# One-row projections of a non-local block as column tiles, with batch statistics from one row per image

## The chip, the cores and the metric

The kernel runs on one NeuronCore of a Trainium2 chip. The metric is device time in microseconds (us) for one execution, the median of several runs. The core has a matrix engine (TensorE, PE), two engines for elementwise work (VectorE, DVE; ScalarE, ACT), GpSimd (POOL) and DMA queues. Tensors in the on-chip memory have 128 partitions; a matmul writes to a separate memory, PSUM[...].

## The reference

The whole kernel is four layers on x of shape (4, 256, 32, 32) in float32: a state-space block, the block treated here, attention with a mixture of experts, and attention with a recurrence of 1024 steps. The change is in layer 1 alone. With N = H*W = 1024 pixels and C = 256 channels it computes

```
g_x     = conv1x1(x, g_w, g_b)          # one output channel: (B, N, 1)
theta_x = conv1x1(x, theta_w, theta_b)  # (B, N, 1)
phi_x   = conv1x1(x, phi_w, phi_b)      # (B, 1, N)
f = matmul(theta_x, phi_x) / N
y = matmul(f, g_x)                      # = theta * (sum over n of phi*g) / N
w_y = conv1x1(y, w_w, w_b)              # C channels: w_w[c]*y + w_b[c]
mean, var = over batch and pixels, per channel
w_y = (w_y - mean) * rsqrt(var + EPS) * bn_gamma + bn_beta
return w_y + x
```

theta, phi and g have one channel each, so y of an image is its theta times one number d, the dot product of phi and g over N. w_y of channel c is then a multiple of that row plus a constant.

## The kernel before, in words

x lies in memory as [128, C=2, B=4, L=1024]: channel c*128+p of image b on partition p. `PHASES` (L1612) calls `_setup`, `_layer0`, `_layer1`, `_layer2`, `_layer3`. A tile framework schedules the instructions of each engine by their dependencies and inserts the semaphores; an engine runs its own list strictly in order. Only the recurrence of layer 3 has an order written out by hand (`_in_order`). Pools of tiles are stacked, so a pool opened by a later phase can lie on memory that an earlier phase has given back; its first writer then waits for the last user.

Layer 0 ends in `_out_and_se` (L439): the pooled mean (L478, L481), two small matmuls (L484, L489), a sigmoid (L491), and L493, eight VectorE instructions of 1024 columns, channel half by channel half and image by image, that add the result to x. ScalarE then issues the load of layer 2's weights, w_l (`_weights`, L178).

`_layer1` (L499) has three steps.

- Projections. L510 spreads each of the six weight columns over 128 columns, so that the matmul (L521) puts the single output channel on all 128 partitions. Eight blocks of W=512 columns, three names and two halves of the contraction make 48 matmuls of 512 columns. ScalarE adds the biases to theta (L525, into y) and phi (L529), and VectorE multiplies g + g_b by phi with an accumulator for the dot product (L530).
- Scaling. The dot products of the two blocks of an image are added (L534, L535) and y of each image is multiplied by its number (L537).
- Batch norm and residual, for each channel half: ScalarE makes w_y over all 4096 columns (L543); `_batchnorm` (L555) takes bn_stats of the eight blocks (L561), aggregates them (L563), and forms scale (L565 to L567); VectorE normalises w_y (L548) and adds it with bn_beta to x (L549).

`_layer2_attention` (L652) follows. `_layernorm` (L184) forms the mean over channels by a matmul with a constant matrix (L196), subtracts it (L197), squares (L199), sums the squares by a matmul (L201), takes a root (L209) and a reciprocal (L211), spreads it by a matmul (L215) and multiplies (L216). `_layer2_weights` (L571) multiplies attention weights into each other (L596, L600, L602) and copies the results (L583 and L603 to L610): these need no x, and the scheduler places them where their inputs allow. `_layer2` prepares constants by small VectorE and POOL instructions (L634 to L644). `_rsqrt` (L911) is a chain of small VectorE instructions, a first guess and four Newton rounds (L930, L932, L934); layers 0 and 2 call it before the change.

A column tile is a matmul with 32 output rows at `tile_position=(0, 32*i)`; it uses 32 of the array's 128 columns and writes PSUM partitions 32*i to 32*i+31. The router in `_head` (L787) and the input gates of layer 3 (L1500) are written in that way already.

Of the kernel before, what the change touches and what calls it, by code (L numbers as in the profile page):

```python
# [10 lines left out]
F32 = mybir.dt.float32  # L11
U32 = mybir.dt.uint32
I32 = mybir.dt.int32
AF = mybir.ActivationFunctionType
ALU = mybir.AluOpType
AX = mybir.AxisListType
PSUM = bass.MemoryType.PSUM

P = 128
B = 4  # L20
L = 1024
T = B * L
D = 256
C = D // P
W = 512
NBLK = T // W
BPI = L // W
# [43 lines left out]
def _bc(ap, axis, n):  # L71

    a = ap.unsqueeze(axis)
    shape = list(a.shape)
    shape[axis] = n
    return a.to_broadcast(shape)
# [421 lines left out]

def _layer1(s):  # L499

    nc, tc = s.nc, s.tc
    with ExitStack() as ctx:
        keep = ctx.enter_context(tc.tile_pool(name="l1_keep", bufs=1))
        pool = ctx.enter_context(tc.tile_pool(name="l1", bufs=2))
        ps = ctx.enter_context(tc.tile_pool(name="l1_ps", bufs=2, space=PSUM))
        wide = {}
        for name in ("theta", "phi", "g"):
            wide[name] = keep.tile([P, C, P], F32, name=f"{name}_wide")
            for k in range(C):
                nc.vector.tensor_scalar_mul(  # L510
                    wide[name][:, k, :], s.ones, s.col[f"{name}_w"][:, k : k + 1]
                )
        y = keep.tile([P, B, L], F32, name="y")
        dot = keep.tile([P, NBLK], F32, name="dot")
        for i in range(NBLK):
            b, t0 = divmod(i * W, L)
            p = {}
            for name in ("theta", "phi", "g"):
                p[name] = ps.tile([P, W], F32, name=f"p_{name}")
                for k in range(C):  # L520
                    nc.tensor.matmul(  # L521
                        p[name], wide[name][:, k, :], s.xt[:, k, bass.ts(i, W)],
                        start=k == 0, stop=k == C - 1,
                    )
            nc.scalar.activation(  # L525
                y[:, b, t0 : t0 + W], p["theta"], AF.Identity, bias=s.row["theta_b"]
            )
            phi = pool.tile([P, W], F32, name="phi")
            nc.scalar.activation(phi, p["phi"], AF.Identity, bias=s.row["phi_b"])  # L529
            nc.vector.scalar_tensor_tensor(  # L530
                phi, p["g"], s.row["g_b"], phi, ALU.add, ALU.mult, accum_out=dot[:, i : i + 1]
            )
        dots = keep.tile([P, B], F32, name="dots")
        nc.vector.tensor_reduce(dots, dot.rearrange("p (b i) -> p b i", i=BPI), AX.X, ALU.add)  # L534
        nc.vector.tensor_scalar_mul(dots, dots, 1.0 / L)  # L535
        for b in range(B):
            nc.vector.tensor_scalar_mul(y[:, b, :], y[:, b, :], dots[:, b : b + 1])  # L537

        yt = y.rearrange("p b l -> p (b l)")
        for c in range(C):  # L540
            wy = pool.tile([P, NBLK, W], F32, name="wy")
            wyt = wy.rearrange("p i w -> p (i w)")
            nc.scalar.activation(  # L543
                wyt, yt, AF.Identity,
                bias=s.col["w_b"][:, c : c + 1], scale=s.col["w_w"][:, c : c + 1],
            )
            mean, scale = _batchnorm(s, pool, wy, s.col["bn_gamma"][:, c : c + 1])
            nc.vector.tensor_scalar(wyt, wyt, mean, scale, ALU.subtract, ALU.mult)  # L548
            nc.vector.scalar_tensor_tensor(  # L549
                s.xt[:, c, :], wyt, s.col["bn_beta"][:, c : c + 1], s.xt[:, c, :],  # L550
                ALU.add, ALU.add,
            )


def _batchnorm(s, pool, v, gamma):  # L555

    nc = s.nc
    n = v.shape[1]
    stats = pool.tile([P, n, nc.vector.BN_STATS_DIM], F32, name=f"bn_stats{n}")
    for i in range(n):  # L560
        nc.vector.bn_stats(stats[:, i, :], v[:, i, :])  # L561
    mv = pool.tile([P, 2], F32, name=f"bn_mv{n}")
    nc.vector.bn_aggr(mv, stats.rearrange("p n d -> p (n d)"))  # L563
    scale = pool.tile([P, 1], F32, name=f"bn_scale{n}")
    nc.scalar.activation(scale, mv[:, 1:2], AF.Sqrt, bias=s.eps)  # L565
    nc.vector.reciprocal(scale, scale)
    nc.vector.tensor_mul(scale, scale, gamma)  # L567
    return mv[:, 0:1], scale
# [772 lines left out]
def _layer3_lstm(s, x, u_l3, lam, add_col):  # L1341
# [269 lines left out]

PHASES = [  # L1612
    _setup, _layer0, _layer1, _layer2, _layer3,
]

# [88 lines left out]
```

## Time and profile before

| | |
|---|---|
| median of three runs | 3567.6 us (3564.02 to 3568.08) |
| the profiled execution | 3564.65 us |
| its span | 3562.9 us |
| busy share of the span | PE 91%, PE weight load 72%, DVE 57%, ACT 35%, POOL 12% |
| mean granted TensorE clock | 0.965 |
| layer 0's last addition to x (L493) | 357.28 to 366.94 us |
| projections of layer 1 (L521) | from 367.28 us |
| y scaled (L537), w_y (L543) | from 411.98 us, from 414.81 us |
| last residual of layer 1 (L549) | from 438.95 us, 4.48 long |
| layer 2's layernorm, first subtraction (L197) | 445.60 us |

A row of the timeline gives the start, the time that the instructions took, engine, line, operation, output and input tiles, and in brackets how long the engine had idled and what released it. A float32 matmul of 512 columns appears as two records. In windows, the numbers are busy time and instructions of PE, PE weight load, DVE, ACT and POOL, then the granted clock, the DMA share and GB/s.

### The profile page before, as it was taken

The numbers are of one execution on the slowest core, as the hardware profiler recorded it, in microseconds if no ns is written. First come the engines' busy times: TensorE is split into PE (matmuls) and PEld (weight loads), VectorE is DVE, ScalarE is ACT, GpSimd is POOL, SyncE is SP. The second block draws the span as 40 slices with busy tenths as digits, with TensorE's granted clock in tenths as the row PEclk, the third lists the DMA queues.
The fourth block names the chain that finished last, engine by engine and source line by source line (L and its number), as shares of the span: only waits on it lengthen the run. The fifth ranks groups of instructions, "written<-read, shape, count | busy, mean of one in ns | idle before, by whom it ended". The sixth has DMA issues, their size and how long they took to land.

```text
span 3562.9 us, 146932 instructions
## 1 busy us (share of the span) xinstructions
PE 3253.3 (91%) x65426; PEld 2549.0 (72%) x65426; DVE 2028.1 (57%) x8373; ACT 1249.5 (35%) x5057; POOL 416.0 (12%) x498
## 2 busy tenths in 40 slices
PE   7786599998899999589999999999999999999888
PEld 4464234445788888357888888888888888888776
DVE  5795544443211111536677777776777777777666
ACT  4623222222222222233334334343343343343333
POOL 0181000113433333200000000000000000000000
PEclk9898789999999999799999999999999999999999
DMA  1390000114455654300000000000000000000000
GB/s 66 88 293 1 9 0 12 36 36 157 175 193 212 223 194 160 125 1 4 5 5 10 4 10 4 5 10 4 4 10 4 10 4 4 10 4 5 10 4 10
DMA packets 79356, 189.32 MB, mean 53 GB/s; under 512 B 6592, under 2 KB 64256, under 8 KB 73728
## 3 DMA queue, kind: packets, MB, share of 16 engines
q0 software_dynamic: 16176, 116.06, 8.9%
q1 hardware_dynamic: 60624, 59.12, 5.6%
q8 instruction: 512, 8.39, 1.0%
q10 hardware_dynamic: 1920, 4.74, 0.4%
q14 instruction: 124, 1.02, 0.1%
HBM read 118.88 MB, written 61.02 MB: 50 GB/s over the span
## 4 chain that ended last, share of the span: by engine, by line
PE 41%; DVE 9%; ACT 4%; issue 2%; ACTq 0%; DVEq 0%
PE p_c L1556 10%; DVE turned L1585 7%; PE p_c L1547 7%; PE p_i L1547 4%; PE p_o L1547 4%; PE p_o L1556 4%; PE p_i L1556 4%; PE beside L1500 4%; ACT a_o L1586 2%; DVE x L1601 2%; ACT th L1599 2%; PE beside L1404 1%; PE beside L1441 0%; PE var L1451 0%; PE p_q L1324 0%
## 5 line engine op out<-in xcount | busy, mean ns | idle before, releaser
L1586 ACT ACTIVATE add<-turned 128x8 f32<-128x8 f32 x1024 | 214.4, 209 | 1027.3 <-DVE turned L1585 1027.3
L1556 PE MATMUL p_c<-w_v,x 128*4 128x64 f32 x16368 | 416.1, 219 | 71.0 <-DVE x L1601 69.0
L1547 PE MATMUL p_c<-xg,shift 128*128 128x64 f32 x2048 | 445.7, 299 | 0.0
L1556 PE MATMUL p_o<-w_v,x 128*4 128x64 f32 x16368 | 416.3, 219 | 0.0
L1556 PE MATMUL p_i<-w_v,x 128*4 128x64 f32 x16368 | 416.1, 219 | 0.0
L1547 PE MATMUL p_i<-xg,shift 128*128 128x64 f32 x2048 | 407.3, 281 | 0.0
L1585 DVE STREAM_TRANSPOSE turned<-p_c 128x64 f32<-128x64 f32 x1024 | 255.7, 250 | 259.0 <-PE p_c L1556 228.0
L1547 PE MATMUL p_o<-xg,shift 128*128 128x64 f32 x2048 | 396.1, 275 | 0.0
L1547 PEld LDWEIGHTS p_c<-xg,shift 128*128 128x128 f32 x2048 | 304.7, 188 | 117.6 <-issue 0.3
L1556 PEld LDWEIGHTS p_c<-w_v,x 128*4 128x4 f32 x16368 | 227.2, 85 | 192.3 <-DVE x L1601 119.1
L1547 PEld LDWEIGHTS p_o<-xg,shift 128*128 128x128 f32 x2048 | 310.9, 192 | 0.3
L1601 DVE TENSOR_TENSOR x<-a_o,th 128x8 f32<-128x8 f32 x1024 | 170.8, 167 | 244.2 <-ACT th L1599 244.2
L1547 PEld LDWEIGHTS p_i<-xg,shift 128*128 128x128 f32 x2048 | 304.7, 188 | 0.4 <-issue 0.3
L1127 PE MATMUL ph<-uT,w 128*128 128x256 f32 x1248 | 282.7, 384 | 16.8 <-DVE uT L1112 12.5
L1141 PE MATMUL po<-w,hT 128*128 128x256 f32 x1248 | 285.5, 382 | 5.6 <-issue 5.0
L1131 ACT ACTIVATE hT<-ph,w 128x256 f32<-128x256 f32 x312 | 147.6, 473 | 398.5 <-PE ph L1127 369.4
L1556 PEld LDWEIGHTS p_o<-w_v,x 128*4 128x4 f32 x16368 | 281.1, 87 | 0.1
L1556 PEld LDWEIGHTS p_i<-w_v,x 128*4 128x4 f32 x16368 | 280.9, 87 | 0.0
L1127 PEld LDWEIGHTS ph<-uT,w 128*128 128x128 f32 x1248 | 238.4, 192 | 54.3 <-DVE uT L1112 16.3
L1585 DVE STREAM_TRANSPOSE turned<-p_i 128x64 f32<-128x64 f32 x1024 | 271.7, 265 | 0.3 <-PE p_i L1547 0.3
L1141 PEld LDWEIGHTS po<-w,hT 128*128 128x128 f32 x1248 | 236.0, 192 | 37.3 <-issue 5.4
L1148 DVE TENSOR_TENSOR y<-po,w 128x256 f32<-128x256 f32 x78 | 33.0, 423 | 392.9 <-PE po L1141 369.6
(409 smaller groups left out, 4678.7 us busy)
## 6 DMA issues: line engine op xcount, KB each, us to landing
sorted<-zeros SPq DMA_DIRECT2D x32, 1032.0 KB
y_in<-results SPq DMA_DIRECT2D x16, 512.0 KB
x<-in_x_dram SPq DMA_DIRECT2D x8, 512.0 KB
tokens<-rows SPq DMA_DIRECT2D x4, 1024.0 KB
x<-tokens SPq DMA_DIRECT2D x8, 512.0 KB
out_dram<-x_l SPq DMA_DIRECT2D x64, 64.0 KB
results<-y,place POOLq DMA_INDIRECT x78
w_l<-in_w_l_dram ACTq DMA_DIRECT2D x1, 1092.0 KB
```

Source lines behind the costliest of these rows:

```text
L1127: nc.tensor.matmul(ph, w1[:, k, bass.ts(n, P)], uT[:, k, :], start=k == 0, stop=k == C - 1,)
L1131: nc.scalar.activation(hT[:, n, :], ph, AF.Gelu, bias=b1[:, n : n + 1])
L1141: nc.tensor.matmul(po, hT[:, n, bass.ts(a, P)], w2[:, n, :], start=n == 0, stop=n == NHC - 1,)
L1148: nc.vector.tensor_add(y, po, b2)
L1404: nc.tensor.matmul(p, lam[:, k, b, bass.ts(m, P)], u_l3[:, k, b * L + n * SB : b * L + (n + 1) * SB], start=k == 0, stop=k == C - 1,)
L1500: nc.tensor.matmul(p[bass.ts(i, R), :], rows[:, k, bass.ts(g, R)], w_u[:, k, at : at + GQ // GC], start=k == 0, stop=k == C - 1, tile_posi ...
L1547: nc.tensor.matmul(p[:, :H], shift[:, row * B : row * B + P], xg[n][:, g, bass.ts(i, H)], start=True, stop=t == 0,)
L1556: nc.tensor.matmul(p[R * i : R * i + B, :H], hs[:, t - 1, bass.ts(k, B)], w_v[:, k, i * GQ + g * H : i * GQ + (g + 1) * H], start=False, s ...
L1585: nc.vector.transpose(zt.rearrange("p c w -> p (c w)"), pz[g][:, :H])
L1586: nc.scalar.activation(dst.rearrange("p (c b) -> p c b", c=C), zt[:, :, :B], f)
L1599: nc.scalar.activation(th, cell[:, :, 1], AF.Tanh)
L1601: nc.vector.tensor_mul(h, a_o, th)
```

## The change

`_layer1` is rewritten; `_batchnorm` stays in use in layer 3.

- theta, phi and g of an image are rows of column tiles. w holds two sets of 32 columns for each half of the contraction: theta and phi in columns 0 and 1 of the first, g in column 1 of the second. Image b goes to column tile b. For each half i of the pixels, p_0 gets theta and phi, p_1 gets g, of all four images: 2 x 2 x 2 x 4 = 32 matmuls of 512 columns. p_0 and p_1 have one PSUM buffer each.
- ScalarE adds both biases in one instruction to rows; bn_stats runs on rows, so that each image's theta row yields mean and variance; VectorE multiplies p_1 + g_b by rows with an accumulator.
- The dot product, mean and variance of each image are placed in columns of own and summed over partitions by a matmul with ones, which gives them to all partitions (every).
- From these, d, the batch mean and the variance of w_y follow by arithmetic on 4 or 2 columns; `_rsqrt` takes the root. coef and off hold each channel's factor for each image and its constant.
- For each image, a matmul with spread puts its theta row on all partitions, in PSUM; ScalarE forms w_y from it with scale and bias (two instructions of 1024 columns), and VectorE adds it to x.

The diff:

```diff
 def _layer1(s):
 
+
     nc, tc = s.nc, s.tc
+    R = P // B
     with ExitStack() as ctx:
         keep = ctx.enter_context(tc.tile_pool(name="l1_keep", bufs=1))
         pool = ctx.enter_context(tc.tile_pool(name="l1", bufs=2))
-        ps = ctx.enter_context(tc.tile_pool(name="l1_ps", bufs=2, space=PSUM))
-        wide = {}
-        for name in ("theta", "phi", "g"):
-            wide[name] = keep.tile([P, C, P], F32, name=f"{name}_wide")
-            for k in range(C):
-                nc.vector.tensor_scalar_mul(
-                    wide[name][:, k, :], s.ones, s.col[f"{name}_w"][:, k : k + 1]
+        ps = ctx.enter_context(tc.tile_pool(name="l1_ps", bufs=1, space=PSUM))
+        wide = ctx.enter_context(tc.tile_pool(name="l1_wide", bufs=2, space=PSUM))
+
+        w = keep.tile([P, 2, C, R], F32, name="w")
+        nc.vector.memset(w, 0.0)
+        for held, row, name in ((0, 0, "theta"), (0, 1, "phi"), (1, 1, "g")):
+            nc.vector.tensor_copy(w[:, held, :, row], s.col[f"{name}_w"])
+        at = s.ident.rearrange("p (b r) -> p r b", r=R)
+        bias = keep.tile([P, 1], F32, name="bias")
+        on = keep.tile([P, 2], F32, name="on")
+        nc.vector.tensor_reduce(on, at[:, :2, :], AX.X, ALU.add)
+        nc.vector.tensor_scalar_mul(bias, on[:, :1], s.row["theta_b"])
+        nc.vector.scalar_tensor_tensor(
+            bias, on[:, 1:], s.row["phi_b"], bias, ALU.mult, ALU.add
+        )
+        spread = keep.tile([P, B, P], F32, name="spread")
+        nc.vector.tensor_copy(spread, _bc(at[:, 0, :], 2, P))
+        w_sq = keep.tile([P, C], F32, name="w_sq")
+        nc.vector.tensor_mul(w_sq, s.col["w_w"], s.col["w_w"])
+
+        rows = keep.tile([P, BPI, W], F32, name="rows")
+        stats = keep.tile([P, BPI, nc.vector.BN_STATS_DIM], F32, name="stats")
+        dot = keep.tile([P, BPI], F32, name="dot")
+        for i in range(BPI):
+            p = [ps.tile([P, W], F32, name=f"p_{j}") for j in range(2)]
+            for j in range(2):
+                for k in range(C):
+                    for b in range(B):
+                        nc.tensor.matmul(
+                            p[j][bass.ts(b, R), :], w[:, j, k, :], s.x[:, k, b, bass.ts(i, W)],
+                            start=k == 0, stop=k == C - 1, tile_position=(0, R * b),
+                        )
+            nc.scalar.activation(rows[:, i, :], p[0], AF.Identity, bias=bias)
+            nc.vector.bn_stats(stats[:, i, :], rows[:, i, :])
+            prod = pool.tile([P, W], F32, name="prod")
+            nc.vector.scalar_tensor_tensor(
+                prod, p[1], s.row["g_b"], rows[:, i, :], ALU.add, ALU.mult,
+                accum_out=dot[:, i : i + 1],
+            )
+        mv = keep.tile([P, 2], F32, name="mv")
+        nc.vector.bn_aggr(mv, stats.rearrange("p n d -> p (n d)"))
+
+        own = keep.tile([P, 3, B], F32, name="own")
+        nc.vector.tensor_scalar_mul(own[:, 0, :], at[:, 1, :], dot[:, :1])
+        for i in range(1, BPI):
+            nc.vector.scalar_tensor_tensor(
+                own[:, 0, :], at[:, 1, :], dot[:, i : i + 1], own[:, 0, :], ALU.mult, ALU.add
+            )
+        for i in range(2):
+            nc.vector.tensor_scalar_mul(own[:, 1 + i, :], at[:, 0, :], mv[:, i : i + 1])
+        p = ps.tile([P, 3, B], F32, name="p_own")
+        nc.tensor.matmul(
+            p.rearrange("p q b -> p (q b)"), s.ones, own.rearrange("p q b -> p (q b)"),
+            start=True, stop=True,
+        )
+        every = keep.tile([P, 3, B], F32, name="every")
+        nc.vector.tensor_copy(every, p)
+        d = keep.tile([P, B], F32, name="d")
+        nc.vector.tensor_scalar_mul(d, every[:, 0, :], 1.0 / L)
+
+        dm = keep.tile([P, B], F32, name="dm")
+        nc.vector.tensor_mul(dm, d, every[:, 1, :])
+        mean = keep.tile([P, 1], F32, name="mean")
+        nc.vector.tensor_reduce(mean, dm, AX.X, ALU.add)
+        nc.vector.tensor_scalar_mul(mean, mean, 1.0 / B)
+        nc.vector.tensor_scalar(dm, dm, mean, None, ALU.subtract)
+        nc.vector.tensor_mul(dm, dm, dm)
+        dv = keep.tile([P, B], F32, name="dv")
+        nc.vector.tensor_mul(dv, d, d)
+        nc.vector.tensor_mul(dv, dv, every[:, 2, :])
+        nc.vector.tensor_add(dv, dv, dm)
+        var = keep.tile([P, 1], F32, name="var")
+        nc.vector.tensor_reduce(var, dv, AX.X, ALU.add)
+        var_c = keep.tile([P, C], F32, name="var_c")
+        nc.vector.tensor_scalar(var_c, w_sq, var, 1.0 / B, ALU.mult, ALU.mult)
+        gain = keep.tile([P, C], F32, name="gain")
+        for _ in _rsqrt(s, pool, gain, var_c):
+            pass
+        nc.vector.tensor_mul(gain, gain, s.col["bn_gamma"])
+        scale = keep.tile([P, C], F32, name="scale")
+        nc.vector.tensor_mul(scale, gain, s.col["w_w"])
+        coef = keep.tile([P, B, C], F32, name="coef")
+        nc.vector.tensor_mul(coef, _bc(d, 2, C), _bc(scale, 1, B))
+
+        off = keep.tile([P, C], F32, name="off")
+        nc.vector.scalar_tensor_tensor(
+            off, s.col["w_w"], mean, s.col["w_b"], ALU.mult, ALU.add
+        )
+        nc.vector.tensor_sub(off, s.col["w_b"], off)
+        nc.vector.tensor_mul(off, off, gain)
+        nc.vector.tensor_add(off, off, s.col["bn_beta"])
+
+        for b in range(B):
+            theta = wide.tile([P, BPI, W], F32, name="theta")
+            for i in range(BPI):
+                nc.tensor.matmul(
+                    theta[:, i, :], spread[:, b, :], rows[:, i, :], start=True, stop=True
                 )
-        y = keep.tile([P, B, L], F32, name="y")
-        dot = keep.tile([P, NBLK], F32, name="dot")
-        for i in range(NBLK):
-            b, t0 = divmod(i * W, L)
-            p = {}
-            for name in ("theta", "phi", "g"):
-                p[name] = ps.tile([P, W], F32, name=f"p_{name}")
-                for k in range(C):
-                    nc.tensor.matmul(
-                        p[name], wide[name][:, k, :], s.xt[:, k, bass.ts(i, W)],
-                        start=k == 0, stop=k == C - 1,
-                    )
-            nc.scalar.activation(
-                y[:, b, t0 : t0 + W], p["theta"], AF.Identity, bias=s.row["theta_b"]
-            )
-            phi = pool.tile([P, W], F32, name="phi")
-            nc.scalar.activation(phi, p["phi"], AF.Identity, bias=s.row["phi_b"])
-            nc.vector.scalar_tensor_tensor(
-                phi, p["g"], s.row["g_b"], phi, ALU.add, ALU.mult, accum_out=dot[:, i : i + 1]
-            )
-        dots = keep.tile([P, B], F32, name="dots")
-        nc.vector.tensor_reduce(dots, dot.rearrange("p (b i) -> p b i", i=BPI), AX.X, ALU.add)
-        nc.vector.tensor_scalar_mul(dots, dots, 1.0 / L)
-        for b in range(B):
-            nc.vector.tensor_scalar_mul(y[:, b, :], y[:, b, :], dots[:, b : b + 1])
-
-        yt = y.rearrange("p b l -> p (b l)")
-        for c in range(C):
-            wy = pool.tile([P, NBLK, W], F32, name="wy")
-            wyt = wy.rearrange("p i w -> p (i w)")
-            nc.scalar.activation(
-                wyt, yt, AF.Identity,
-                bias=s.col["w_b"][:, c : c + 1], scale=s.col["w_w"][:, c : c + 1],
-            )
-            mean, scale = _batchnorm(s, pool, wy, s.col["bn_gamma"][:, c : c + 1])
-            nc.vector.tensor_scalar(wyt, wyt, mean, scale, ALU.subtract, ALU.mult)
-            nc.vector.scalar_tensor_tensor(
-                s.xt[:, c, :], wyt, s.col["bn_beta"][:, c : c + 1], s.xt[:, c, :],
-                ALU.add, ALU.add,
-            )
+            for c in range(C):
+                wy = pool.tile([P, L], F32, name="wy")
+                nc.scalar.activation(
+                    wy, theta.rearrange("p i w -> p (i w)"), AF.Identity,
+                    bias=off[:, c : c + 1], scale=coef[:, b, c : c + 1],
+                )
+                xs = s.x[:, c, b, :]
+                nc.vector.tensor_add(xs, xs, wy)
 
 
 def _batchnorm(s, pool, v, gamma):
```

## The prediction

> **What bounds the kernel now.** I first read the table of windows for the stretch between the end of layer 0 and layer 2's layernorm, then its timeline.[...]
>
> ```profile
> 366.90:372.00 5.10, 4.72 (x7) 2.15 (x8) 1.21 (x7) 0.69 (x1) 0.00 (x0) 0.58 0.00 0
> 372.00:411.70 39.70, 38.78 (x92) 16.90 (x90) 6.19 (x17) 10.30 (x15) 0.00 (x0) 1.00 0.00 0
> 411.70:443.50 31.80, 7.37 (x29) 4.46 (x29) 27.45 (x46) 9.36 (x5) 0.18 (x1) 0.62 0.00 0
> ...
> 447.00:473.10 26.10, 26.04 (x64) 7.53 (x64) 8.72 (x11) 8.37 (x8) 0.00 (x0) 1.00 0.00 0
> ```
>
> Layer 1 has two parts, each with one engine full: TensorE to 411.7 (43.5 of 44.8 us), then VectorE (27.5 of 31.8). The ends of the parts are in the timeline (start, us, engine, line):
>
> ```profile
> 357.28 9.66 DVE L493 SCALAR_TENSOR_TENSOR x<-o,att,x 128x1024 f32<-128x1024 f32 x8 [2.42 <-ACT att L491]
> ...
> 410.79 0.75 DVE L530 SCALAR_TENSOR_TENSOR phi<-p_g,rows,phi 128x512 f32<-128x512 f32 x1 [4.39 <-PE p_g L521]
> ...
> 414.81 7.49 ACT L543 ACTIVATE wy<-y,cols 128x4096 f32<-128x4096 f32 x2 [5.12 <-DVE y L537]
> ...
> 427.32 2.40 DVE L548 TENSOR_SCALAR wy<-wy,bn_mv,bn_scale 128x4096 f32<-128x4096 f32 x1
> ...
> 438.95 4.48 DVE L549 SCALAR_TENSOR_TENSOR x<-wy,cols,x 128x4096 f32<-128x4096 f32 x1
> ...
> 445.60 2.52 DVE L197 TENSOR_TENSOR u<-x,mean 128x1024 f32<-128x1024 f32 x2 [0.60 <-PE mean L196]
> ```
>
> From layer 0's last residual (357.28 + 9.66 = 366.94) to layernorm's first subtraction (445.60) are **78.7 us**, and nothing else runs beside them: POOL has 0.35 us of work, the DMA share is 0.00. Everything later needs x, so what this stretch loses or gains goes to the end of the span.
>
> Prices come from the answer on the tile wg (durations min/median/max, first and last start) and from the groups, with shapes kept apart (count, busy us, mean ns):
>
> ```profile
> L787 PE MATMUL p_head<-x,wg x16: 379/379/403, 889.1 to 889.8; 128*32 128x256 f32 x16
> ```
>
> ```profile
> L241 ACT ACTIVATE acc<-xbc,cols 128x1024 f32<-128x1024 f32 x16 | 19.7, 1238 | 0.3
> ```
>
> ```profile
> L197 DVE TENSOR_TENSOR u<-x,mean 128x1024 f32<-128x1024 f32 x8 | 9.8, 1221 | 15.2 <-PE mean L196 15.1
> ...
> L932 DVE TENSOR_TENSOR e<-e,rstd 128x8 f32<-128x8 f32 x32 | 5.3, 166 | 1.1
> ```
>
> The first is the router's matmul in column tiles: a source matmul is two records, so 8 matmuls of 256 columns are 16 records. Full-width records of 512 columns follow each other at 0.43 us (L521), so 256 columns cost 0.215 and 16 in a row 3.4 us; they start within 0.7 us and end after 1.07. Four column tiles do run abreast.
>
> [...] granted clock 0.51 while VectorE adds the residual (357.3 to 366.9), 1.00 from 372. [...]
>
> **The change part by part**, on the clock of the profiled run (before: 366.94 to 445.60).
>
> *Preparation.* Eight small VectorE instructions (w, on, spread, bias, w_sq) stand in the built order between pooled and the first L493. VectorE idled 2.42 us there. One 128x512 copy (0.42 at L605), two of about 0.17 and five of 0.15 to 0.2 make 1.8, and the memset of w waits some 0.5 us for TensorE to let go of the layer 0 weights under it. I take +0.2; bounds 0 (all hidden) and +1.8 (no cover). The six L510 multiplies go; the first of them stood on the path, 0.3.
>
> *Matmuls.* 48 full-width matmuls of 0.86 (two records of 0.43) become 32 tiled ones. The built order matters: the first half (16, i=0) goes image by image as p_0, p_1 on the same column tile, each pair released by one L493, which come every 1.21. A pair is 1.72, but p_1 of one image can lie beside p_0 of the next, so at full clock TensorE keeps up and only the last image's pair is left: p_0 ends at 367.1 + 0.86 + 0.17 = 368.2 (a record lasts 0.59, 0.17 beyond its 0.43). At half clock the first pairs fall behind[...]. p_0 has one buffer, so i=1 waits for ScalarE to empty it: 0.69 (L525), 368.9. Then 8 tiled matmuls four abreast, 2 x 0.86 + 0.17 = 1.9: 370.8. p_1 waits in the same way for VectorE: bn_stats 0.68 (L561) and prod 0.83 (L530 with its accumulator read), which end at 370.5; its matmuls end at 372.5. The second prod and own: 0.83 + 0.2, 373.5. Then p_own; it is queued behind two theta matmuls of image 0 (1.72 from 372.4), so 374.6 with its copy's start. Layer 2's bb, wv and bv (L605 and neighbours, 0.9) now sit in VectorE's queue ahead of the first bn_stats, in the shadow of that wait; wv waits for the w_l2 load, which was issued at 357.8 and whose 0.79 MB had moved by 367. Bounds of this part: 4 us more if the clock is still half at the end, 2 less if the halves meet better.
>
> *Statistics chain.* 35 small VectorE instructions from every to off. A chain in the trace steps by 0.20 per dependent instruction (four Newton rounds of L930, L932, L934 at 14.82 to 17.22), 0.08 for an independent one. 28 dependent steps are 5.6, 7 others 0.6. The scheduler puts mat, r, wv and bv between them: 0.68 + 0.45. r waits for small, which TensorE reaches after theta of image 1 (1.7) and the 3.5 us of L596: about 380, and VectorE stands some 0.8. Sum 8.1: coef and off at **382.7**. Bounds 7 and 12 (0.3 per step).
>
> *Residual by image.* ScalarE writes wy from PSUM (1.23), VectorE adds (1.22), two buffers: a period of 1.3 with the semaphores, so 1.23 + 7 x 1.3 + 1.24 = 11.6. Theta of images 2 and 3 waits until ScalarE has emptied a buffer; TensorE has then idled over 4 us, as before L215's half-clock records (0.86 apart at 477), so these 4 records take 3.4 instead of 1.7 and arrive some 2 us late. 13.6: x is complete at **396.3**. Bounds 10 and 15.
>
> *Into layernorm.* The means of blocks 0, 1 and half of 2 are then done, so after about 1.0 us of small instructions that stand ahead (pair, first, go_on) the first L197 starts at **397.3**; six more small ones behind it delay the second by some 0.4. From there the 27.5 us to the root (445.60 to 473.1) repeat; they alternate mean, square and variance. The table load for Sqrt moves to L209 (1.28), where ScalarE waits 2.0 for the variance: nothing.
>
> *Removed with this:* scaling y (2.7), two wy passes (7.5), 16 bn_stats less two, L548 and L549 over 4096 columns (4.8 + 8.9).
>
> **Sum.** 445.6 - 397.3 = 48.3, less 0.4: **48 us**. The profiled run took 3564.65 (span 3562.9 and 1.75 around it), so 3516.7. The median before, 3567.6, is 2.95 higher, inside the runs' own 4 us; from it the sum gives 3519.6. I take **3518**.
>
> **Rivals.**
> 1. *512-column tiles don't overlap*[...]. For it: L787 has only 256 columns, and the first half pairs matmuls on one tile. Against: the 4-fold rate above. 32 x 0.86 = 27.5 from 358.6 to 386 in place of 372.5, saving 34: about 3532.
> 2. *Latency chain*: 35 steps at 0.3 and cold theta twice over, 4 + 2 us more, saving 42: about 3525. [...]against: the steady 0.20.
> 3. *Better overlap*: no cold theta, no stall for small, less in the chain; 5 us more: 3512.
> 4. *Slower: the recurrence at a lower clock.* PE lines of the LSTM loop (L1556, L1547, L1500) are 38% of the chain, about 1370 us, at a granted clock of 0.99 to 1.00 after 1600. [...] If it fell to c, the loop would gain at most 1370 x (1/c - 1): 48 us at 0.966, and the result is slower by 0.2% (3575) from 0.961. For: 0.95 in the windows from 900 to 1600. Against: that loop has no long idle.
> 5. *The change doesn't do what it says:* only i=1 has all four images abreast; this is in the sum.
>
> **Chances.** Forecast (3513 to 3523) 0.66, rival 3 (3506 to 3513) 0.10, rival 2 (3523 to 3529) 0.11, rival 1 (3529 to 3540) 0.08, rival 4 with slower 0.02 and lost gain 0.03. The range 3507 to 3531 leaves out under 0.2. Faster by over 0.2% (7 us, about what a measurement here can tell from none) 0.96; within 0.02; slower 0.02.
>
> **What would show it.** L535's last records near 372, four abreast for i=1; off near 382.7; eight adds (L612) 1.2 to 1.3 apart, with one gap before image 2; L197 near 397; later stages of the same length. Wrong if L535 takes over 20 us, if small steps exceed 0.25, or if the stretch from the root to the end changes by over 5 us.

## The result, and the profile after

The changed kernel takes **3512.97 us** (median; 3509.8 to 3514.82) against 3565.81 (3560.08 to 3568.08) for the kernel before in the same session: ratio 0.9856, 95% interval 0.9844 to 0.9868. The forecast was 3518 with a range of 3507 to 3531. The profiled execution took 3514.67 us, span 3512.7, mean clock 0.969; its span is 50.2 us shorter than that of before, where the sum said 48.

The windows over layer 1 come first (columns as before). Lines below L499 have moved by up to 60: the expert matmul L1127 of before is L1187, the recurrence's L1585 is L1645.

```profile
366.90:372.00 5.10, 5.10 (x35) 1.37 (x37) 2.65 (x9) 1.38 (x2) 0.00 (x0) 1.00 0.00 0
372.00:383.40 11.40, 8.85 (x50) 6.01 (x42) 7.63 (x46) 1.13 (x2) 0.00 (x0) 0.92 0.01 2
383.40:394.60 11.20, 6.85 (x11) 2.90 (x12) 9.45 (x10) 8.07 (x8) 0.18 (x1) 0.77 0.00 0
394.60:422.90 28.30, 27.53 (x62) 7.45 (x60) 10.51 (x25) 9.73 (x9) 0.18 (x1) 1.00 0.00 0
```

The two long one-engine parts of before (43.5 us of TensorE, then 27.5 of VectorE) are gone. What is left are three short pieces with different limits: 5 us of matmuls, 11 us in which VectorE works through small steps, 11 us in which ScalarE and VectorE hand each other w_y. In the third the clock is 0.77. The last window is layernorm, again full of TensorE work.

The timeline of the same kernel shows the pieces' ends. A first fence for the projections:

```profile
357.47 9.66 DVE L493 SCALAR_TENSOR_TENSOR x<-o,att,x 128x1024 f32<-128x1024 f32 x8 [0.71 <-ACT att L491]
...
358.90 13.79 PE L535 MATMUL p<-x,w 128*32 128x512 f32 x64 [1.03 <-DVE x L493]
...
368.31 0.69 ACT L539 ACTIVATE rows<-p,bias 128x512 f32<-128x512 f32 x1 [10.14 <-PE p L535]
...
371.04 0.69 ACT L539 ACTIVATE rows<-p,bias 128x512 f32<-128x512 f32 x1 [2.04 <-PE p L535]
...
374.77 0.17 DVE L563 COPY every<-p_own 128x12 f32<-128x12 f32 x1 [0.75 <-PE p_own L558]
```

All 32 projection matmuls (64 records) lie between 358.90 and 372.7; the projections of before began at 367.28 and ran to 410.7. Half of them now lie beside L493. L493 starts 0.19 later than before, but so does the instruction ahead of the preparation, first in the trace of before, then of the changed kernel:

```profile
354.69 0.17 DVE L481 TENSOR_SCALAR pooled<-pooled 128x8 f32<-128x8 f32 x1
```

```profile
354.88 0.17 DVE L481 TENSOR_SCALAR pooled<-pooled 128x8 f32<-128x8 f32 x1
```

From there to L493 are 2.59 us in both, so of the preparation's nine small steps nothing is seen on the path: VectorE's wait ahead of L493 has shrunk from 2.42 to 0.71. The second half needs 2.0 us from p_0's release (368.31 + 0.69) to the next ACTIVATE at 371.04.

Next the statistics chain, and the residual with the start of layernorm:

```profile
379.20 0.69 DVE L663 COPY mat<-pm 128x512 f32<-128x512 f32 x1
...
379.81 0.15 DVE L994 SCALAR_TENSOR_TENSOR gain<-e,gain 128x2 f32<-128x2 f32 x1
...
380.89 0.16 DVE L664 COPY r<-small 128x2 f32<-128x2 f32 x1 [0.93 <-PE small L662]
...
382.02 0.15 DVE L597 TENSOR_TENSOR off<-off,cols 128x2 f32<-128x2 f32 x1
382.27 2.30 ACT L607 ACTIVATE wy<-theta,off,coef 128x1024 f32<-128x1024 f32 x2 [10.54 <-DVE off L597]
383.50 2.36 DVE L612 TENSOR_TENSOR x<-x,wy 128x1024 f32<-128x1024 f32 x2 [1.33 <-ACT wy L607]
...
384.62 5.59 PE L602 MATMUL theta<-rows,spread 128*128 128x512 f32 x8 [3.77 <-ACT wy L607]
...
389.68 2.36 DVE L612 TENSOR_TENSOR x<-x,wy 128x1024 f32<-128x1024 f32 x2 [1.25 <-ACT wy L607]
...
392.23 2.36 DVE L612 TENSOR_TENSOR x<-x,wy 128x1024 f32<-128x1024 f32 x2 [0.20 <-ACT wy L607]
...
393.35 4.56 PE L196 MATMUL mean<-x,avg 128*128 128x512 f32 x10 [3.13 <-ACT wy L607]
...
395.37 1.22 DVE L197 TENSOR_TENSOR u<-x,mean 128x1024 f32<-128x1024 f32 x1 [0.40 <-PE mean L196]
```

Read the brackets. VectorE waits 0.93 for small, 1.33 for the first w_y, 1.25 ahead of image 2, 0.20 ahead of the other pairs, 0.40 for layernorm's first mean. The second bracket on PE matters later: the first mean matmul was released not by x, but by the last w_y. That instruction writes nothing that the mean needs, but it is the last reader of theta, so what it gave back is a PSUM buffer.

From here the times by kernel are compared in one table. The end of L493 moves by up to 1.4 us between these traces, so each mark is counted from the end of layer 0's last addition (L493) of the same trace: start of every, end of off, then the starts of the first subtraction of layernorm (L197), its root (L209) and the first matmul of the experts. The times are medians; the kernel before took 3563.0 to 3567.8 in the same sessions.

| kernel | every | off | first L197 | root | experts | time, us |
|---|---|---|---|---|---|---|
| before | | | 78.7 | 106.2 | 485.1 | 3565.8 |
| changed | 7.6 | 15.0 | 28.2 | 55.8 | 434.7 | 3513.0 |
| changed, again | 7.6 | 15.0 | 28.2 | 55.8 | 434.7 | 3511.8 |
| full-width weights | 33.8 | 41.2 | 54.4 | 82.0 | 461.8 | 3545.8 |
| preparation behind | 11.4 | 18.8 | 32.1 | 60.8 | 440.1 | 3519.8 |
| statistics and residual alone | | 52.3 | 59.9 | 87.6 | 464.8 | 3545.8 |
| tiles alone | | | 45.4 | 73.5 | 451.4 | 3533.8 |
| theta early | 7.7 | 13.4 | 21.6 | 51.3 | 430.7 | 3508.2 |
| copies on ScalarE | 7.6 | 13.4 | 27.0 | 54.6 | 434.2 | 3511.8 |
| all three edits | 8.0 | 13.7 | 20.1 | 51.5 | 430.6 | 3509.2 |
| own first | 6.5 | 15.9 | 25.0 | 52.7 | 431.0 | 3511.0 |

The change gains 106.2 - 55.8 = 50.4 us by layernorm's root and keeps 50.4 at the first expert matmul.

### The profile page after: what moved, and what is told of

It is laid out like the page before. It is cut to its first block, busy times and chain, and to the rows that moved or that the text cites. A ratio compares the mean times of both kernels' runs of the same rounds, so it can differ in the third digit from the quotient of the medians.

```text
span 3512.7 us, 146893 instructions
## 1 busy us (share of the span) xinstructions
PE 3227.6 (92%) x65412; PEld 2536.4 (72%) x65412; DVE 2016.5 (57%) x8382; ACT 1245.0 (35%) x5047; POOL 416.3 (12%) x498
## 4 chain that ended last, share of the span: by engine, by line
PE 41%; DVE 9%; ACT 4%; issue 2%; ACTq 0%; DVEq 0%
PE p_c L1616 11%; DVE turned L1645 7%; PE p_c L1607 7%; PE p_i L1607 4%; PE p_o L1607 4%; PE p_i L1616 4%; PE p_o L1616 4%; PE beside L1560 4%; ACT a_o L1646 2%; DVE x L1661 2%; ACT th L1659 2%; PE beside L1464 1%; PE beside L1501 0%; PE var L1511 0%; PE p_q L1384 0%
## 5 line engine op out<-in xcount | busy, mean ns | idle before, releaser
L1645 DVE STREAM_TRANSPOSE turned<-p_c 128x64 f32<-128x64 f32 x1024 | 255.9, 250 | 257.1 <-PE p_c L1616 226.7
L1187 PE MATMUL ph<-uT,w 128*128 128x256 f32 x1248 | 284.6, 386 | 20.8 <-DVE uT L1172 20.7
L1187 PEld LDWEIGHTS ph<-uT,w 128*128 128x128 f32 x1248 | 240.4, 194 | 58.2 <-DVE uT L1172 24.6
L1645 DVE STREAM_TRANSPOSE turned<-p_i 128x64 f32<-128x64 f32 x1024 | 271.6, 265 | 0.7 <-PE p_i L1607 0.3
L1645 DVE STREAM_TRANSPOSE turned<-p_o 128x64 f32<-128x64 f32 x1024 | 256.0, 250 | 0.3 <-PE p_o L1616 0.3
## 6 DMA issues: line engine op xcount, KB each, us to landing
w_l<-in_w_l_dram ACTq DMA_DIRECT2D x1, 1092.0 KB, 11.4
```

What stands on the lines that cost most here:

```text
L1187: nc.tensor.matmul(ph, w1[:, k, bass.ts(n, P)], uT[:, k, :], start=k == 0, stop=k == C - 1,)
L1645: nc.vector.transpose(zt.rearrange("p c w -> p (c w)"), pz[g][:, :H])
```

## Experiments

The theory was that of the prediction. The rivals were tiles that don't overlap, a dearer chain, and a change in the later stages.

**1. The same work without column tiles.** Every weight column set is padded with zeros to 128 columns, so each matmul is full width and the images add up in one PSUM tile. The number of matmuls is the same. The padded w is larger, and its preparation falls behind L493.

```diff
-        w = keep.tile([P, 2, C, R], F32, name="w")
+        Z = R * (B - 1)
+        w = keep.tile([P, 2, C, 2 * Z + R], F32, name="w")
...
-                            p[j][bass.ts(b, R), :], w[:, j, k, :], s.x[:, k, b, bass.ts(i, W)],
-                            start=k == 0, stop=k == C - 1, tile_position=(0, R * b),
+                            p[j], w[:, j, k, Z - R * b : Z - R * b + P], s.x[:, k, b, bass.ts(i, W)],
+                            start=k == 0 and b == 0, stop=k == C - 1 and b == B - 1,
```

> The changed kernel with its 32 projection matmuls over the full 128 columns (weights padded with zeros, the four images accumulated into one bank) instead of column tiles; the larger weight tile lies on other memory, so that the preparation falls behind the last residual of layer 0, as in e7_prep_behind, with which it is to be compared. Theory (four tiles run abreast): each of the four groups of 8 matmuls takes 6.9 us instead of 1.7, so the second prod starts near 398.6 us instead of 377 in e7, 21 us later; total about 3539. Rival (the gain comes from 32 matmuls in place of 48, and the tiles run one after another[...]): within 1 us of e7_prep_behind.

**2. The preparation behind L493.** An unused tile of 16 KB per partition moves w onto memory that the second matmul ahead of the sigmoid (L489) reads last; TensorE reaches that only when L493 is next on VectorE (357.30 and 357.28 in the trace of before).

```diff
+        room = ctx.enter_context(tc.tile_pool(name="l1_room", bufs=1))
+        unused = room.tile([P, B, L], F32, name="unused")
+        nc.vector.memset(unused[:, 0, :1], 0.0)
```

> The changed kernel with an unused tile of 16 KB per partition in front of its tiles, which moves the weight tile to memory whose last reader is the second matmul of the sigmoid; the scheduler then puts the preparation of w, bias and spread behind the eight additions of layer 0. Theory of the prediction (cover gone: preparation on the path and no matmul beside the additions): 1.2 us until w is ready, and two more groups of 8 tiled matmuls after the last x, partly at half clock; the second prod 4 us later than the changed kernel's 373.0; total about 3517. Rival (the small instructions cost nothing wherever they stand): 3513 or less than 1 us more.

Measured: 3545.75 us for the first (ratio 0.9936, 0.9919 to 0.9953), 3519.83 for the second (0.9868, 0.9852 to 0.9885; 3517 expected). Both have the preparation behind L493, so they differ in the tiles and in the longer preparation of the padded w. TensorE in the timeline of the kernel with full-width weights:

```profile
368.45 30.35 PE L536 MATMUL p<-x,w 128*128 128x512 f32 x64 [10.63 <-DVE w L514]
```

and of the kernel with the preparation behind:

```profile
367.96 8.44 PE L538 MATMUL p<-x,w 128*32 128x512 f32 x64 [9.89 <-DVE w L516]
376.33 1.98 PE L605 MATMUL theta<-rows,spread 128*128 128x512 f32 x4
```

The same 64 records take 30.35 us full width and 8.44 in tiles, 3.6 times less, waits for p_0 and p_1 included. That settles rival 1. Full-width theta starts at 376.33, and the last tiled record ends at 376.40 (367.96 + 8.44): a cost of going from tiles to full width, if any, is too small to see (the ends of matmuls are modelled). The two kernels differ by 22.5 us at every (21 expected); 0.7 of that is the preparation, since the projections start 1.58 us after L493 full width and 0.84 in tiles. At the root they differ by 21.1, for a reason that comes next. The times lie 25.9 apart, and the first is 7 above the 3539 that was expected: from the first expert matmul to the end of the span its profile shows 2717.5 us against 2710.5, with nothing edited there.

The second kernel against the changed one prices the cover: **3.7 us** at every and at off (4 expected for the second product), though its diff adds one idle tile and a one-column memset. The preparation itself is 1 us; the rest is that no projection can start before it, so the first half's matmuls lie in the open. By the root the loss is 5.0 us. The other 1.2 of it arise between the first L197 and the root (28.8 us against 27.5; the second L197 comes 2.93 after the first, 399.21 to 402.14, against 1.72, 395.37 to 397.09), where TensorE's weight loads of the mean, which all take 0.19 us there in the changed kernel, grow longer for four records:

```profile
397.67 0.19 PEld L196 LDWEIGHTS mean<-x,avg 128*128 128x128 f32 x1 [0.24 <-issue]
398.11 0.34 PEld L196 LDWEIGHTS mean<-x,avg 128*128 128x128 f32 x1 [0.25 <-issue]
```

The granted clock from 399 to 402 is 0.59. So this part is the clock in the next stage, and not the cover. In the time the two are 6.9 us apart, in sessions in which the kernel before differed by 2.0.

**3. Statistics and residual alone.** The projections of before with all of y kept, then per-image statistics and the residual image by image; no p_own is needed, since each partition holds every image's row. The diffs of experiments 3 and 4 are against the changed kernel.

```diff
-            nc.scalar.activation(rows[:, i, :], p[0], AF.Identity, bias=bias)
-            nc.vector.bn_stats(stats[:, i, :], rows[:, i, :])
+            nc.scalar.activation(
+                y[:, b, t0 : t0 + W], p["theta"], AF.Identity, bias=s.row["theta_b"]
+            )
+            nc.vector.bn_stats(stats[:, i, :], y[:, b, t0 : t0 + W])
...
-                    wy, theta.rearrange("p i w -> p (i w)"), AF.Identity,
+                    wy, y[:, b, :], AF.Identity,
```

> The kernel before with its own 48 full-width projections, but statistics from each image's theta and the residual added image by image as in the change. Theory (the two gains add up): saves the second half only: the last prod ends at 411.6 as before, the chain of small steps takes about 8 us with the stall for layer 2's small products, the residual 11; 15 us less than before, about 3551. Rival (nearly all of the gain belongs to the projections, the batch norm being as long in small steps as in wide ones): under 5 us less, 3561 or more.

**4. Tiles alone.** The projections of the changed kernel; then y is written out and normalised and added as before.

```diff
+            nc.scalar.activation(
+                y[:, b, :], theta.rearrange("p i w -> p (i w)"), AF.Copy, scale=d[:, b : b + 1]
+            )
...
+            mean, scale = _batchnorm(s, pool, wy, s.col["bn_gamma"][:, c : c + 1])
```

> The changed kernel's tiled projections, then y written out for all images and the batch norm and residual of the kernel before (w_y over 4096 columns, 16 bn_stats, L548, L549). Theory: y is ready at 380.9 us instead of 414.8, so 34 us less than before, about 3532; with e2_stats_residual's 15 that makes the 50 of the whole change. Rival (the gains need each other, since the theta rows must be spread over the partitions again): 25 us or less, 3541 or more.

Measured: 3545.84 us (0.9943, 0.9926 to 0.9959) and 3533.79 (0.9905, 0.9889 to 0.9922). The first was expected at 3551, the second at 3532. By the root the statistics alone give 106.2 - 87.6 = 18.6 us, the tiles alone 32.7; together 51.3, and the whole change 50.4. The two halves of the change nearly add.

The tiles did as expected (34.0 us of time). The statistics gave more than the 15 expected (21.9 in the time), and VectorE's timeline of that kernel shows why:

```profile
426.28 1.23 DVE L586 TENSOR_TENSOR x<-x,wy 128x1024 f32<-128x1024 f32 x1 [0.18 <-ACT wy L581]
427.43 1.22 DVE L197 TENSOR_TENSOR u<-x,mean 128x1024 f32<-128x1024 f32 x1
428.56 2.35 DVE L586 TENSOR_TENSOR x<-x,wy 128x1024 f32<-128x1024 f32 x2
```

Layernorm starts between the additions. There is no theta in PSUM there, TensorE is free (it idles 6.00 us ahead of the first mean at 422.49), and the means of the first images run while the last are being added. From off to the root this kernel takes 87.6 - 52.3 = 35.3 us, the changed one 40.7. That 5.5 us was lost in the changed kernel, and the next experiments look for it.

**5. Theta early.** All four theta rows are spread and copied to memory during the statistics chain; w_y is made from memory.

```diff
+        y = rest.tile([P, B, L], F32, name="y")
+        for b in range(B):
+            theta = wide.tile([P, BPI, W], F32, name="theta")
...
+            nc.scalar.copy(y[:, b, :], theta.rearrange("p i w -> p (i w)"))
...
-                    wy, theta.rearrange("p i w -> p (i w)"), AF.Identity,
+                    wy, y[:, b, :], AF.Identity,
```

> Edit: all four theta rows are spread and copied by ScalarE to memory while VectorE works through the statistics chain, so that w_y is made from memory and no theta matmul is left behind the chain. What is tried: two waits that the changed kernel shows behind the chain, 1.31 us of VectorE ahead of image 2 (its theta runs at half clock and after ScalarE has freed a buffer) and 0.40 us on the mean ahead of the first subtraction of layernorm, whose first matmul starts only at 393.35, when the last theta gives back its PSUM. My theory (these are real waits on the path): off stays at 382.0 to 382.4, the eight additions follow each other at 1.2 to 1.25 us without a gap, the means start before the last addition, and the time falls by 1.7 us, to 3511.3, or by 2 to 4 if subtractions of layernorm get in between the additions as they did where before's projections were kept. Rival (VectorE is the bound of the stretch from the first addition to the root, and the gap only moves): first subtraction earlier, but the root at the same time as in the changed kernel within 0.5 us, and no change of the time, 3513. Slower by 1 to 3 us if the copies on ScalarE delay off or the first w_y.

**6. Layer 2's copies on ScalarE.** mat, r and the column of wv and bv leave VectorE's chain.

```diff
-    nc.vector.tensor_copy(s.mat, pm)
-    nc.vector.tensor_copy(s.r, pr)
+    nc.scalar.copy(s.mat, pm)
+    nc.scalar.copy(s.r, pr)
...
-    nc.vector.tensor_scalar_mul(s.wv[:, :, D], pc, scale)
+    nc.scalar.mul(s.wv[:, :, D], pc, scale)
...
-    nc.vector.tensor_scalar_mul(s.bv[:, D:], pb, scale)
+    nc.scalar.mul(s.bv[:, D:], pb, scale)
```

> Edit: the four copies of layer 2's weights (mat, r, wv, bv) that stand in the middle of the statistics chain are taken by ScalarE, which is idle there. What is tried: the term of 1.13 + 0.8 us that the prediction put on these copies and their wait. My theory (the chain is VectorE's own order and the copies stand on its path: 0.69 for mat, 0.93 of waiting for small, the rest short): off comes 1.8 to 2.2 us earlier, near 380.1, the first subtraction near 393.4, the time 3511. Rival (theta is late next): image 1's theta is queued on TensorE behind the products of layer 2 that the copies belong to, so the first additions come earlier and the gap ahead of image 1 or 2 grows by as much; off earlier by 2 and the last addition by less than 0.7; 3512.5.

**7. Both, and two PSUM buffers for p_0 and p_1** (theta then has one):

```diff
+        ps2 = ctx.enter_context(tc.tile_pool(name="l1_ps2", bufs=2, space=PSUM))
...
-        wide = ctx.enter_context(tc.tile_pool(name="l1_wide", bufs=2, space=PSUM))
+        wide = ctx.enter_context(tc.tile_pool(name="l1_wide", bufs=1, space=PSUM))
...
-            p = [ps.tile([P, W], F32, name=f"p_{j}") for j in range(2)]
+            p = [ps2.tile([P, W], F32, name=f"p_{j}") for j in range(2)]
```

> Edit: the two edits above together, and two PSUM buffers each for p_0 and p_1, so that the second half of the pixels need not wait for ScalarE and VectorE to empty the first half's buffers. What is tried: the 0.69 + waiting for p_1's buffer, about 1.5 us at most by the trace of the changed kernel (last matmul of the projections at 371.9, against 367.1 for the last x and 3.6 us for the sixteen matmuls of the second half, which can begin at once), and whether the gains add. My theory: all three are on one path and add: 1.7 + 2.0 + 1.0 to 1.5, every near 373.5, off near 380.8 or earlier, time 3508 to 3509. Rival: the half-granted clock at the end of layer 0 makes the first half's pairs fall behind in any case, so buffers bring nothing: 3509.5.

**8. The changed kernel again**, with no edit.

> Edit: none, the changed kernel once more. What is tried: how much of the 50.2 us between the two profiled executions is the stretch of layer 1 (50.23 at the first subtraction of layernorm) and how much scatter of the later stages. My theory: the time within 2 us of 3513, the first subtraction at 395.4 within 0.2, while the length of the expert stage and of the recurrence (576.4 and 1938.2 us in the first profile, 579.1 and 1933.9 before) moves by 1 to 4 us in either direction with no edit made. Rival (the change moves the later stages itself): both lengths within 0.5 us of the first profile of this kernel.

These four ran together (before: 3563.0). Times and ratios: theta early 3508.2 us (0.985, 0.9837 to 0.9863), copies 3511.84 (0.986, 0.9844 to 0.9875), all three 3509.23 (0.9854, 0.9839 to 0.9869), changed kernel 3511.78 (0.9857, 0.9842 to 0.9873). These intervals overlap, so the times alone don't rank the four; the marks do. The changed kernel's repeat has every mark of layer 1 within 0.1 us of the first profile, which is what the marks of the others are read against. Its recurrence was 1935.5 us from the first to the last L1645, against 1938.2 in the first profile, while the expert stage (L1187) stayed at 576.5 against 576.4: of the two stretches that were expected to move by 1 to 4 us, one did.

*Theta early* gains 4.5 us by the root (55.79 to 51.32) and 4.0 at the experts; at both it is level with all three edits within 0.2 us, and ahead of the other kernels. Its VectorE timeline:

```profile
380.66 0.15 DVE L606 TENSOR_TENSOR off<-off,cols 128x2 f32<-128x2 f32 x1
382.18 1.23 DVE L616 TENSOR_TENSOR x<-x,wy 128x1024 f32<-128x1024 f32 x1 [1.37 <-ACT wy L611]
383.32 0.69 DVE L667 COPY mat<-pm 128x512 f32<-128x512 f32 x1
...
388.99 1.22 DVE L197 TENSOR_TENSOR u<-x,mean 128x1024 f32<-128x1024 f32 x1 [1.82 <-PE mean L196]
390.13 2.35 DVE L616 TENSOR_TENSOR x<-x,wy 128x1024 f32<-128x1024 f32 x2
```

off comes 1.65 earlier, which was not expected: the products of layer 2 are now behind all theta matmuls, so the copy of mat falls out of the chain. The additions were expected without a gap; there is a new one (1.82, for the first mean). So 1.65 of the gain is the earlier off. The other 2.8 came by the way that the expectation named second, the subtractions between the additions: from off to the root it is 37.9 us, between the 40.7 of the changed kernel and the 35.3 of experiment 3. The copy of mat and a wait of 0.61 for small stand between the additions now; they and the 1.82 are gaps that experiment 3 doesn't have there.

*The copies* took 1.65 us out of the chain (off 13.4 instead of 15.0), a little under the 1.8 to 2.2 of the theory, but only 1.2 are left at the root and 0.5 at the experts. ScalarE's queue shows the first loss:

```profile
381.17 0.16 ACT L664 COPY r<-small 128x2 f32<-128x2 f32 x1 [1.05 <-PE small L662]
...
381.34 2.31 ACT L607 ACTIVATE wy<-theta,off,coef 128x1024 f32<-128x1024 f32 x2
```

off was ready at 380.80; w_y stood behind r, wv and bv in ScalarE's list until 381.34. The wait for small did not go away; it moved to the engine that is next on the path. The gap ahead of image 2 stayed (1.31). The time is that of the changed kernel, but the rival's reason isn't shown: it wanted a gap grown by as much as off came earlier and the last addition earlier by less than 0.7, and the last addition ends 1.2 earlier (26.3 us after L493 instead of 27.5). The loss between the root and the experts (0.7) stays open.

*All three* gained nothing over theta early. own was complete 5.75 us after L493 instead of 6.9, and every came no earlier. TensorE's timeline of that kernel:

```profile
370.06 1.98 PE L568 MATMUL theta<-rows,spread 128*128 128x512 f32 x4
373.14 1.13 PE L568 MATMUL theta<-rows,spread 128*128 128x512 f32 x2 [1.10 <-ACT y L571]
374.10 0.29 PE L560 MATMUL p_own<-own,ones 128*128 128x12 f32 x2
```

p_own, on which the chain waits, is queued behind a theta matmul that waits for ScalarE's copy. The time is the rival's (3509.5), but the forecast rival (first half falling behind at half clock) is not what did it.

**9. own first.** Theta early with the two buffers, and p_own taken from theta's own PSUM buffer, so that no theta can stand ahead of it.

```diff
-        p = ps.tile([P, 3, B], F32, name="p_own")
+        p = wide.tile([P, BPI, W], F32, name="theta")[:, 0, : 3 * B]
+        p = p.rearrange("p (q b) -> p q b", b=B)
```

> Edit: the kernel with theta early, plus two PSUM buffers each for p_0 and p_1, with p_own taken from theta's own PSUM buffer so that no theta can stand ahead of it on TensorE; layer 2's copies are on VectorE again. What is tried: why two buffers brought nothing in the kernel that had all three edits. There own was complete 1.1 us earlier (5.75 us after layer 0's last addition, against 6.89), but every came no earlier (7.98 against 7.64), since p_own was queued behind theta of image 1, which waited for ScalarE. My theory (TensorE's order ate the gain): own near 5.7 us after the last addition, p_own 0.4 to 1.3 later, every at 6.5 to 7.1, so 0.6 to 1.1 us earlier than in the kernel with theta early (7.65), and layernorm's root as much earlier, if the single theta buffer doesn't delay w_y; time 3507.3. Rival (the additions wait for theta instead: with one PSUM buffer the four copies are not done when off is ready): root at the same time as with theta early (52.0 us from the last addition to the reciprocal) or later, 3508.2 to 3510.

Measured: 3510.99 us (before 3565.63; 0.9844, 0.9831 to 0.9858). Half of the theory holds: every comes at 6.5, 1.1 us earlier, so the order on TensorE was what ate the gain. In the result the rival was right: the root at 52.7 is 1.3 later than with theta early. Its reason is there too, since the last two of the four copies start only after off (385.73 and 388.90 against 383.2). But it is not what costs the time: from off to the root are 36.7 us, fewer than the 37.9 of theta early. What is late is off itself (15.9):

```profile
373.79 0.17 DVE L565 COPY every<-theta 128x12 f32<-128x12 f32 x1 [0.71 <-PE theta L560]
...
379.05 0.69 DVE L668 COPY mat<-pm 128x512 f32<-128x512 f32 x1 [2.13 <-PE pm L661]
```

VectorE stands 2.13 us in the middle of the chain for pm, whose last matmul is queued behind theta of image 0, at a clock of 0.72 (372.5 to 378.5). The copy of mat is back in the chain, and worse than before.

## Why the prediction was right, and where its sizes were off

- **Preparation** (+0.2): nothing; the 0.19 by which L493 starts later was there ahead of it. There are nine steps, not eight, and they take 1.1 us (355.66 to 356.76) and not 1.8. The wait of w for TensorE was 0.61 (0.5 forecast). That it all hides rests on where w lies in memory; experiment 2 takes that away for 3.7 us at every, more than the stated bound of 1.8, since the bound left out the matmuls that wait behind the preparation. The prediction's bound failed there.
- **Matmuls**: rows[0] at 368.31 (368.2), second ACTIVATE 371.04 (370.8), every 374.77 (374.6): within 0.3 us. The second prod starts 0.5 late (373.01; 372.5), behind the aggregation and two steps of own on VectorE, and own is complete at 374.0 (373.5). That cost little, because the forecast had p_own wait for theta until 374.1 in any case. Four 512-column tiles run abreast, as argued from L787's 256 columns (8.44 us against 30.35 in experiments 2 and 1). The first half ran at a granted clock of 0.52 from 358.9 to 364.8, with TensorE busy throughout, and at 1.00 from 365.2, so ahead of the last x.
- **Statistics chain** (8.1 to off): 374.77 to 382.17 is 7.4. The kernel without the copies prices the rest: 375.05 to 380.80, 5.75, where 5.6 + 0.6 was forecast (the independent steps fill the 0.20 between dependent ones and cost next to nothing). The copies and the wait are then 1.65, not 1.93.
- **Residual by image** (13.6): 382.17 to 394.59 is 12.4. The cold theta is real (a granted clock of 0.50 from 384.6 to 388.2), but costs 1.05 us (a gap of 1.25, where the other pairs have 0.20) and not 2. The prediction put the whole excess of half clock (1.7) and a little more on the path. Theta of image 2 starts at 384.62, with w_y of image 1 (384.82 to 387.12) running beside it; at full clock it would have had some 0.5 us to spare there (an estimate: theta of image 0 took 1.98 at a clock of 1.00, from 372.62), and that part of the excess is free. TensorE had idled 3.77 us ahead of 384.62, and from there about 4 us passed until the weight loads of L602 grow short:

```profile
388.19 0.33 PEld L602 LDWEIGHTS theta<-rows,spread 128*128 128x128 f32 x1 [0.52 <-issue]
388.76 0.19 PEld L602 LDWEIGHTS theta<-rows,spread 128*128 128x128 f32 x1 [0.24 <-issue]
```

By image 3 the clock was back (1.00 from 388.7 to 390.5). In the kernel before, L521's weight loads grow short 4.2 us after its start (367.25 to 371.46); with L535, 5.9 us of work were still at 0.52. No fixed time until the full clock is shown. The pairs of additions start 2.56 us apart, so the period is 1.28 as forecast (1.3); from off on, that part is 0.2 less than the 11.6.

- **Into layernorm** (1.0): 0.78. This one was right by accident. The prediction had the means of two and a half blocks done beforehand; in fact none was, since the first mean matmul waits until the last w_y frees theta's PSUM (393.35). The small VectorE steps then covered most of it, and 0.40 was left. Experiment 3 and theta early, where the means do run ahead, need 5.5 and 2.8 us less from off to the root: that gain of early means, subtractions between the additions, was in no term of the prediction. The 0.4 of later loss did not come: from the first L197 to the root are 27.5 us, as before.
- **Sum**: preparation 0.2, off 0.5 early, residual 1.2, layernorm 0.2, no later loss 0.4: 2.5 us, and 47.9 + 2.5 = 50.4 is what the marks show. The span shows 50.2, since everything ahead of L493 took 0.2 longer in this execution.
- **The base.** 3518 is 5.0 above the median: 1.3 is the step from 3516.7 up to 3518, 2.0 is what the profiled execution took less than 3516.7, and 1.7 is what it lay above the median. So the median of 3512.97 falls just below the forecast's own 3513 to 3523 and in rival 3's 3506 to 3513, to which 0.10 was given. That is chance and not its mechanism: the cold theta and the wait for small, which it left out, are both there; only its third point, less in the chain, came true in part (0.7).
- **Later stages.** From the first expert matmul to the end of the span are 2711.0 us before and 2710.9 after. The same stretch took 2707.9 in the changed kernel's repeat and 2708.0 to 2717.5 in the other kernels, with nothing edited there. That scatter is larger than what is left to explain, and what sets it stays open. Rival 4 (the recurrence at a lower clock) did not occur: the clock over the recurrence is 1.00 in both profiles, while its length differs by 4.3 us (1938.2 against 1933.9).

A ladder sums up where the 50.4 us came from, at the root: one row per image in place of 128 copies, with statistics and residual by image, 24.2 (before to experiment 1); tiles abreast, 21.1 (1 to 2); cover beside L493, 5.0 (2 to the changed kernel). Of the first step, 11.9 are there by the start of the last product (43.9 us after L493 before, 32.0 in experiment 1), from 32 matmuls in place of 48; how the rest divides between the statistics and the residual no run separates. The last two steps are 22.5 and 3.7 if they are read at every, ahead of the slow mean matmuls of experiment 2.

## What to carry to other kernels

Price each engine's list, not only its busy time: three times here a gain was eaten because the instruction that mattered stood behind one that waited (p_own behind theta, w_y behind r, the chain behind mat), and each time the wait had only changed its engine. When a step is to hide beside earlier work, find out whose memory it writes; 3.7 us, and 5.0 with what followed, hung on the place of one small tile. And ask who frees the PSUM buffer that the next stage needs: a stage whose inputs are ready still starts with the last reader of the buffer it gets (the first mean at 393.35, released by the last w_y).

## What the runs showed of the hardware beyond expectation

- Thirty-two float32 matmuls of 32 output rows and 512 columns, four tiles abreast, took 8.44 us against 30.35 for the same ones at full width, 3.6 times less, with no visible cost for going from tiles to full width (376.33 and 376.40 in experiment 2).
- Small VectorE steps of 2 or 4 columns follow each other at 0.195 us when each needs the last, and an independent step fits between two of them: 35 steps took 5.75 us.
- VectorE additions of 1024 columns are listed as 1.22 us each, but two in a row take 2.36: in a sum, 1.14 is the price of the second.
